# Pairwise bilinear products: the second tile of a two-tile x load is issued by GpSimd and placed on chosen DMA engines

## The chip, the cores and the metric

The kernel runs on one core of one Trainium2 chip. The metric is device time in microseconds (us). The time before is 1336.77 us, the median of three runs (1336.71 to 1336.96). A profiled execution has a span of 1335.1 us, counted from the first to the last instruction.

A core has five engines with their own instruction streams: TensorE (PE; its weight loads are listed apart as PEld), VectorE (DVE), ScalarE (ACT), GpSimd (POOL) and SyncE (SP). Sixteen DMA engines move data between HBM and the core's memory SBUF. SyncE, ScalarE and GpSimd can each issue transfers, and each has its own queue.

## The reference

The input has 4096 samples of 32 fields with 64 numbers each. For every pair of fields i < j (496 pairs) field i of each sample is multiplied by a 64 x 64 matrix that belongs to the pair, and the result is multiplied element by element with field j:

```python
i_idx, j_idx = np.triu_indices(32, k=1)
vi = inputs[:, i_idx, :]
vj = inputs[:, j_idx, :]
vdotw = jnp.einsum('bpd,pde->bpe', vi, W)     # W: (496, 64, 64)
return (vdotw * vj).reshape(B, -1)            # (4096, 31744) float32
```

All is float32. The output is 520 MB, the input x 33.6 MB, the weights 8.4 MB (with padding). So the kernel is mostly a stream of stores.

## The kernel before

The samples lie in 32 tiles (NT) of 128 rows, one row for each partition. For a tile, TensorE transposes x, multiplies each pair of fields (2p, 2p + 1) with the weights of all later fields into PSUM, and VectorE multiplies PSUM with x into a ring buffer in SBUF, from which SyncE stores. There are four stores in a tile, 7552, 6528, 7872 and 9792 columns wide; the ring has 28160 columns.

```python
STORES = [[0, 1], [2, 3], [4, 5, 6], [7, 8, 9, 10, 11, 12, 13, 14, 15]]
FIRST_HALF_AT, SECOND_HALF_AT = 9, 3
RING = 28160

def x_slots(NT):                       # which tiles are loaded together, and into which slot
    loads = [[(0, 0)]]
    for t in range(1, NT, 2):
        if t + 1 == NT:
            loads.append([(t, 1)])
        elif loads[-1][-1] == (t - 1, 2):
            loads.append([(t + 1, 0), (t, 1)])
        else:
            loads.append([(t, 1), (t + 1, 2)])
    return loads
...
    xbuf = const.tile([P, 3 * F * D], F32, tag="x", name="x")     # three slots of one tile
    def load_x(load):
        at = sum(len(before) for before in x_loads[: x_loads.index(load)]) * P * F * D
        n = len(load) * F * D
        s = load[0][1]
        nc.scalar.dma_start(
            out=xbuf[:, s * F * D : s * F * D + n],
            in_=x[at : at + P * n].rearrange("(p c) -> p c", p=P),
        )
...
    for t in range(NT):
        xt = slot[t]
        for load in x_loads:
            if min(load)[0] == t + 1:
                load_x(load)
        for s, group in enumerate(STORES):
            if at + store_w[s] > RING:
                at = 0
            osb = ring[:, at : at + store_w[s]]
            at += store_w[s]
            for p in group:
                if p == SECOND_HALF_AT:
                    transpose_x(xt, 1)
                if p == FIRST_HALF_AT and t + 1 < NT:
                    transpose_x(slot[t + 1], 0)
                ...                      # matmuls into PSUM, then on VectorE:
                        nc.vector.tensor_tensor(
                            runs(osb, o[0], o[1], n), runs(pm, 0, BANK, n), ..., ALU.mult)
            nc.sync.dma_start(
                out=out[:, t * cols + o0 : t * cols + o0 + store_w[s]], in_=osb
            )
```

x comes in 17 loads: tile 0 alone, fifteen loads of two tiles, and tile 31 alone. In a two-tile load each partition gets one run of 16 KB. The host lays x out so that each load is contiguous in HBM.

Of the kernel before, what the change touches and what calls it, by code (L numbers as in the profile page):

```python
# [1 line left out]

# [6 lines left out]

F32 = mybir.dt.float32  # L10
ALU = mybir.AluOpType

P = 128
BANK = 512
BANKS = 8

STORES = [[0, 1], [2, 3], [4, 5, 6], [7, 8, 9, 10, 11, 12, 13, 14, 15]]

LOADS = [[0], [1], [2, 3], [4, 5, 6], [7, 8, 9, 10, 11, 12, 13, 14, 15]]


FIRST_HALF_AT, SECOND_HALF_AT = 9, 3
RING = 28160


def x_slots(NT):
# [13 lines that stand above are left out]
@with_exitstack  # L40
def pair_bilinear_kernel(
    ctx: ExitStack,
    tc: tile.TileContext,
    x: bass.AP,
    w: bass.AP,
    out: bass.AP,
    F: int,
    D: int,
):

    nc = tc.nc
    NT = out.shape[1] * 2 // (F * (F - 1) * D)
    NPR = F // 2

    width = [(F - 1 - i) * D for i in range(F)]
    off = [sum(width[:i]) for i in range(F)]
    cols = sum(width)  # L80


    woff = [i % 2 * D + sum(width[i % 2 : i : 2]) for i in range(F)]
    store_w = [sum(width[2 * p] + width[2 * p + 1] for p in g) for g in STORES]

    const = ctx.enter_context(tc.tile_pool(name="const", bufs=1))
    psum = ctx.enter_context(tc.tile_pool(name="ps", bufs=1, space=bass.MemoryType.PSUM))

    ident = const.tile([P, P], F32, tag="ident", name="ident")
    make_identity(nc, ident)  # L90

    def runs(tl, a, b, n):

        ap = tl[:, a : a + n]
        return bass.AP(ap.tensor, ap.offset, [list(ap.ap[0]), [b - a, 2], list(ap.ap[1])])

    xbuf = const.tile([P, 3 * F * D], F32, tag="x", name="x")
    x_loads = x_slots(NT)
    slot = {t: xbuf[:, ts(s, F * D)] for load in x_loads for t, s in load}

    def load_x(load):

        at = sum(len(before) for before in x_loads[: x_loads.index(load)]) * P * F * D
        n = len(load) * F * D
        s = load[0][1]
        nc.scalar.dma_start(
            out=xbuf[:, s * F * D : s * F * D + n],
            in_=x[at : at + P * n].rearrange("(p c) -> p c", p=P),
        )

    pring = psum.tile([P, BANKS * BANK], F32, tag="pring", name="pring")
    bank = 0

    def take_banks(n):

        nonlocal bank
        if bank + n > BANKS:
            bank = 0
        got = pring[:, bank * BANK : (bank + n) * BANK]
        bank = (bank + n) % BANKS  # L120
        return got

    xT = const.tile([P, NPR * P], F32, tag="xT", name="xT")

    def transpose_x(xt, g):

        n = 2 * BANK // P
        pt = take_banks(2)
        for c in range(n):
            nc.tensor.transpose(pt[:, ts(c, P)], xt[:, ts(n * g + c, P)], ident)  # L130
        nc.scalar.copy(xT[:, ts(g, 2 * BANK)], pt)  # L131

    ring = const.tile([P, RING], F32, tag="ring", name="ring")
    at = 0

    load_x(x_loads[0])
    w_sb = const.tile([P, sum(width[0::2])], F32, tag="w", name="w")
    done = 0
    for g in LOADS:

        upto = woff[2 * g[-1]] + width[2 * g[-1]]
        nc.sync.dma_start(out=w_sb[:, done:upto], in_=w[:, done:upto])
        done = upto

    transpose_x(slot[0], 0)
# [10 lines that stand above are left out]
            o0 = off[2 * group[0]]  # L156
# [5 lines that stand above are left out]
                first = (width[2 * p] - 1) % BANK + 1  # L162
                for c1 in range(first, width[2 * p] + 1, BANK):
                    n = first if c1 == first else BANK
                    c0 = c1 - n
                    odd = width[2 * p + 1] and c1 > D
                    pm = take_banks(2)
                    for h in range(1 + bool(odd)):
                        a = woff[2 * p + h] + c0 - h * D
                        nc.tensor.matmul(  # L170
                            pm[:, h * BANK : h * BANK + n],
                            xT[h * D : (h + 1) * D, ts(p, P)],
                            w_sb[h * D : (h + 1) * D, a : a + n],
                            start=True,
                            stop=True,
                        )
                    xj = xt[:, (2 * p + 1) * D + c0 : (2 * p + 1) * D + c1]
                    o = [off[2 * p + h] - o0 + c0 - h * D for h in range(2)]
                    if odd and (c0 or c1 < width[2 * p]):
                        nc.vector.tensor_tensor(  # L180
                            runs(osb, o[0], o[1], n),
                            runs(pm, 0, BANK, n),
                            bass.AP(xj.tensor, xj.offset, [xj.ap[0], [0, 2], xj.ap[1]]),
                            ALU.mult,
                        )
                    else:
                        for h in range(1 + bool(odd)):
                            nc.vector.tensor_tensor(  # L188
                                osb[:, o[h] + h * D : o[h] + n],
                                pm[:, h * (BANK + D) : h * BANK + n],  # L190
                                xj[:, h * D :],
                                ALU.mult,
                            )
            nc.sync.dma_start(
                out=out[:, t * cols + o0 : t * cols + o0 + store_w[s]], in_=osb
            )


# [30 lines left out]
```

## Time and profile before

| | before |
|---|---|
| time, median of three | 1336.77 us |
| span of the profiled execution | 1335.1 us |
| DMA traffic | 562.87 MB in 21659 packets, mean 422 GB/s |
| stores, a tile | four, 3264 to 4896 KB, median 17.7 to 18.6 us from issue to landing |
| two-tile x load | 2048 KB, median 20.4 us from issue to landing |
| GpSimd | 0.7 us busy, no transfers |

How to read the lines that follow. In the list of busy times each engine has its time, the share of the span and the number of instructions. In the line of slices the span is cut into 40, and each digit is the busy share in tenths. A DMA queue has packets, MB and the time that its packets took as a share of sixteen engines' span. The chain is the work that ended last, followed back from the end. In the list of waits a line names who waited for whom, then the total in us, how often, and the longest. In a table of windows each row is a stretch of the span: its length, the busy time of PE, PEld, DVE, ACT and POOL with the number of instructions, the granted TensorE clock, the share of time in which DMA engines were busy, and GB/s.

### The profile page before, as it was taken

The page shows a single profiled execution, that of the slowest core. Times are in us where ns is not written, and L with a number is a line of the kernel's source. Part 1 is how long each engine was busy: PE and PEld are TensorE (multiplying, and loading weights), DVE is VectorE, ACT ScalarE, POOL GpSimd, SP SyncE. Part 2 cuts the span into 40 slices and gives each one's busy share as a digit, 9 for nine tenths or more (in the row PEclk, how much of TensorE's full clock was granted, in tenths as well). Part 3 has the DMA queues.
Part 4 walks back from the last instruction along what each step waited for, and adds up shares of the span by engine and source line. Part 5 has one row for each costly group of instructions (what it writes and reads, how often), then busy time and mean ns, then how long its engine had stood idle before and what let it go on. Part 6 is the DMA issues. An engine that isn't in the chain of part 4 may idle for free.

```text
span 1335.1 us, 13080 instructions
## 1 busy us (share of the span) xinstructions
PE 1160.6 (87%) x5376; PEld 544.9 (41%) x5376; DVE 1183.4 (89%) x1376; ACT 66.1 (5%) x65; POOL 0.7 (0%) x6
## 2 busy tenths in 40 slices
PE   6998989989899898998989889798998979989893
PEld 3443334443344443444444444344443434354441
DVE  5998989989899898998989899898998989989894
ACT  0000000000000000000000000000000000000000
POOL 0000000000000000000000000000000000000000
PEclk9999999989899999998989999899999999989997
DMA  9999999999999999999999999999999999999998
GB/s 397 433 430 430 431 428 430 418 433 430 413 425 410 436 414 427 426 414 433 405 432 431 419 429 411 432 426 421 428 413 430 426 407 417 429 421 423 429 425 352
DMA packets 21659, 562.87 MB, mean 422 GB/s; under 512 B 2400, under 2 KB 2400, under 8 KB 2656
## 3 DMA queue, kind: packets, MB, share of 16 engines
q1 hardware_dynamic: 19152, 528.49, 92.8%
q10 hardware_dynamic: 2448, 33.56, 5.9%
q8 instruction: 42, 0.69, 0.2%
q14 instruction: 17, 0.14, 0.0%
HBM read 41.94 MB, written 520.09 MB: 421 GB/s over the span
## 4 chain that ended last, share of the span: by engine, by line
DMA 47%; DVE 38%; issue 9%; PE 5%; DVEq 0%; ACT 0%
DMA out_dram<-ring 46%; DVE ring L180 32%; DVE ring L188 5%; PE pring L170 5%; DMA x<-in_x_dram 1%; DVEq L180 0%; PE pring L130 0%; ACT xT L131 0%; DVEq L225 0%; DVEq L188 0%
## 5 line engine op out<-in xcount | busy, mean ns | idle before, releaser
L170 PE MATMUL pring<-w,xT 64*128 64x512 f32 (+4 forms) x4864 | 1098.4, 564 | 146.4 <-DVE ring L180 133.5
L180 DVE TENSOR_TENSOR ring<-pring,x 128x1024 f32<-128x1024 f32 (+3 forms) x1056 | 1104.1, 1108 | 131.4 <-DMA out_dram<-ring 102.6
L170 PEld LDWEIGHTS pring<-w,xT 64*128 64x128 f32 x4864 | 489.3, 191 | 711.7 <-DVE ring L180 533.0
L131 ACT COPY xT<-pring 128x1024 f32<-128x1024 f32 x64 | 64.8, 1012 | 1224.1 <-PE pring L130 1224.1
L188 DVE TENSOR_TENSOR ring<-pring,x 128x64 f32<-128x64 f32 (+3 forms) x320 | 97.7, 356 | 2.6 <-DMA out_dram<-ring 1.9
L130 PEld LDWEIGHTS pring<-ident,x 128*128 128x128 f32 x512 | 55.6, 142 | 58.8 <-DVE ring L180 50.2
L130 PE MATMUL pring<-ident,x 128*128 128x128 f32 x512 | 70.8, 282 | 8.6 <-DMA x<-in_x_dram 8.6
L131 ACT ACT_TABLE_LOAD x1 | 1.3, 1283 | 1.7 <-PEq L221 1.7
masks.py:199 POOL TENSOR_SCALAR_AFFINE_SELECT ident<-ident 128x128 f32<-128x128 f32 x1 | 0.3, 292 | 0.1
masks.py:197 POOL MEMSET ident<- 128x128 f32 x1 | 0.2, 204 | 0.3 <-POOLq L221 0.3
L221 POOL MEMSET const-bfloat16-1.0<- 128x1 bf16 x1 | 0.1, 101 | 0.0
L221 POOL MEMSET const-uint8-127<- 128x1 uint8 x1 | 0.1, 101 | 0.0
L221 POOL MEMSET const-float32-0.0<- 128x1 f32 x1 | 0.1, 98 | 0.2 <-issue 0.2
L221 POOL MEMSET const-float32-1.0<- 128x1 f32 x1 | 0.1, 98 | 0.0
## 6 DMA issues: line engine op xcount, KB each, us to landing
out_dram<-ring SPq DMA_DIRECT2D x32, 4896.0 KB, 17.7
out_dram<-ring SPq DMA_DIRECT2D x32, 3936.0 KB, 18.1
out_dram<-ring SPq DMA_DIRECT2D x32, 3776.0 KB, 18.3
out_dram<-ring SPq DMA_DIRECT2D x32, 3264.0 KB, 18.6
x<-in_x_dram ACTq DMA_DIRECT2D x15, 2048.0 KB, 20.4
w<-in_w_dram SPq DMA_DIRECT2D x1, 2592.0 KB, 28.1
x<-in_x_dram ACTq DMA_DIRECT2D x2, 1024.0 KB, 12.8
w<-in_w_dram SPq DMA_DIRECT2D x1, 2016.0 KB, 22.2
```

Of the source, the lines that this page charges most:

```text
L130: nc.tensor.transpose(pt[:, ts(c, P)], xt[:, ts(n * g + c, P)], ident)
L131: nc.scalar.copy(xT[:, ts(g, 2 * BANK)], pt)
L170: nc.tensor.matmul(pm[:, h * BANK : h * BANK + n], xT[h * D : (h + 1) * D, ts(p, P)], w_sb[h * D : (h + 1) * D, a : a + n], start=True, st ...
L180: nc.vector.tensor_tensor(runs(osb, o[0], o[1], n), runs(pm, 0, BANK, n), bass.AP(xj.tensor, xj.offset, [xj.ap[0], [0, 2], xj.ap[1]]), ALU ...
L188: nc.vector.tensor_tensor(osb[:, o[h] + h * D : o[h] + n], pm[:, h * (BANK + D) : h * BANK + n], xj[:, h * D :], ALU.mult,)
L221: nc = bacc.Bacc("TRN2", target_bir_lowering=False, num_devices=1)
```

## The change

Thirteen of the fifteen two-tile loads, those whose second tile is 2, 4, ..., 26, are split. Their odd tile still comes from ScalarE. The even tile is issued by GpSimd in two transfers: 120 rows that are to lie on fifteen DMA engines, all but engine 4, and the last 8 rows on two engines, a pair that rotates from load to load. [...]so small transfers of k rows ("nudges", 16-byte pieces into a scratch tile that nothing reads) are put ahead of them to move the start to where it is wanted. The idea behind it is that one of the sixteen DMA engines has other work besides and should carry less of x.

```diff
+DMA_ENGINES = 16
+LIGHT = 4
+LIGHT_TILES = range(2, 28, 2)
+PAIRS_FROM = [6, 8, 10, 12, 14, 0, 1]
+HEAD = P - P % (DMA_ENGINES - 1)      # 120 rows
+REST = (P - HEAD) // 2                # 4 rows for each of two engines
+PAD = 16
...
+    def from_pool(out, in_):
+        tc.keep_in_program_order(nc.gpsimd.dma_start(out=out, in_=in_))
+
+    def from_engine(e):
+        nonlocal cursor
+        k = (e - cursor) % DMA_ENGINES
+        if k:
+            nudge = nudges[e == LIGHT + 1]
+            from_pool(
+                nudge[:k].rearrange("p (h c) -> p h c", h=2)[:, :, :4],
+                x[: k * 8].rearrange("(p h c) -> p h c", p=k, h=2),
+            )
+        cursor = e
+
+    def load_beside(at, xt, lap):
+        nonlocal cursor
+        n = F * D
+        from_engine(PAIRS_FROM[lap % len(PAIRS_FROM)])
+        g = REST * n + PAD
+        tail = x[at + HEAD * n : at + HEAD * n + 2 * g].rearrange("(g c) -> g c", g=2)
+        from_pool(xt[HEAD:], tail[:, : REST * n])
+        cursor += 2
+        from_engine(LIGHT + 1)
+        from_pool(
+            xt[:HEAD].rearrange("p (h c) -> p h c", h=2),
+            x[at : at + HEAD * n].rearrange("(h p c) -> p h c", h=2, p=HEAD),
+        )
+        cursor = LIGHT
+
     def load_x(load):
-        at = sum(len(before) for before in x_loads[: x_loads.index(load)]) * P * F * D
-        n = len(load) * F * D
-        s = load[0][1]
-        nc.scalar.dma_start(
-            out=xbuf[:, s * F * D : s * F * D + n],
-            in_=x[at : at + P * n].rearrange("(p c) -> p c", p=P),
-        )
+        at = sum(x_sizes[: x_loads.index(load)])
+        parts = [[(t, s)] for t, s in load] if any(t in LIGHT_TILES for t, s in load) else [load]
+        for part in parts:
+            t, s = part[0]
+            n = len(part) * F * D
+            if t in LIGHT_TILES:
+                load_beside(at, slot[t], LIGHT_TILES.index(t))
+            else:
+                nc.scalar.dma_start(
+                    out=xbuf[:, s * F * D : s * F * D + n],
+                    in_=x[at : at + P * n].rearrange("(p c) -> p c", p=P),
+                )
+            at += P * n + (2 * PAD if t in LIGHT_TILES else 0)
```

The host's layout of x follows (not shown): of an even tile the 120 rows are stored as two halves of 4 KB a row, the 8 rows as two blocks of four rows with 16 numbers of padding behind each. TensorE, VectorE and SyncE have the same instructions in the same order as before; ScalarE has 17 x loads as before, thirteen of them half as large; GpSimd has 52 transfers that it did not have.

More of the change, by code (lines that the diff above doesn't have):

```diff
@@ L98, in pair_bilinear_kernel @@
     x_loads = x_slots(NT)
+    x_sizes = [
+        sum(P * F * D + (2 * PAD if t in LIGHT_TILES else 0) for t, s in load) for load in x_loads
+    ]
     slot = {t: xbuf[:, ts(s, F * D)] for load in x_loads for t, s in load}
-    def load_x(load):
-        at = sum(len(before) for before in x_loads[: x_loads.index(load)]) * P * F * D
-        n = len(load) * F * D
-        s = load[0][1]
-        nc.scalar.dma_start(
-            out=xbuf[:, s * F * D : s * F * D + n],
-            in_=x[at : at + P * n].rearrange("(p c) -> p c", p=P),
-        )
+    nudges = [const.tile([DMA_ENGINES, 16], F32, tag=f"nudge{i}", name=f"nudge{i}") for i in range(2)]
+    cursor = 0
+    def from_pool(out, in_):
[24 more added lines that the diff above has]
+        cursor = LIGHT
+    def load_x(load):
+        at = sum(x_sizes[: x_loads.index(load)])
[11 more added lines that the diff above has]
+            at += P * n + (2 * PAD if t in LIGHT_TILES else 0)
     pring = psum.tile([P, BANKS * BANK], F32, tag="pring", name="pring")
@@ L209 @@
     rows = r_inputs.reshape(P, NT, F * D)
-    x = np.concatenate([rows[:, [t for t, _ in load]].ravel() for load in x_slots(NT)])
+    x = []
+    for load in x_slots(NT):
+        tiles = [t for t, _ in load]
+        if not any(t in LIGHT_TILES for t in tiles):
+            x.append(rows[:, tiles].ravel())
+            continue
+        for t in tiles:
+            if t in LIGHT_TILES:
+                x.append(rows[:HEAD, t].reshape(HEAD, 2, -1).transpose(1, 0, 2).ravel())
+                tail = np.zeros((2, REST * F * D + PAD), rows.dtype)
+                tail[:, : REST * F * D] = rows[HEAD:, t].reshape(2, -1)
+                x.append(tail.ravel())
+            else:
+                x.append(rows[:, t].ravel())
+    x = np.concatenate(x)
     wt = np.transpose(L0_rec_W, (1, 0, 2))
```

## The prediction

> **What bounds the kernel now.** I read the page's busy times first, then the DMA slices and queues, then the chain and the list of waits, and last the waits and windows cut into stages.
>
> ```profile
> PE 1160.6 (87%) x5376; PEld 544.9 (41%) x5376; DVE 1183.4 (89%) x1376; ACT 66.1 (5%) x65; POOL 0.7 (0%) x6
> DMA  9999999999999999999999999999999999999998
> q1 hardware_dynamic: 19152, 528.49, 92.8%
> q10 hardware_dynamic: 2448, 33.56, 5.9%
> q8 instruction: 42, 0.69, 0.2%
> ...
> DMA 47%; DVE 38%; issue 9%; PE 5%; DVEq 0%; ACT 0%
> ```
>
> VectorE is busy for 1183.4 of 1335.1 us, so some 150 us are left over; the DMA engines are in use from the first slice to the last. The store queue q1 and the x queue q10 take 98.7% of sixteen engines' span. The chain agrees: its largest part is the stores. So the bound is the DMA engines, and what counts is how evenly the work lies on the sixteen. The queue list has the hint: q8 is not data but instruction blocks, 42 of 16 KB, and 0.69 MB over TensorE's 2 x 5376 instructions is 64 bytes each.
>
> The list of waits, in two stages, shows how much room VectorE has. First 41 to 205 us (four tiles), then 205 to 1312 us (27 tiles):
>
> ```profile
> DVE ring L180 <- DMA out_dram<-ring: 13.0, 6, 5.1
> ...
> DVE ring L180 <- DMA out_dram<-ring: 89.7, 38, 6.2
> ```
>
> VectorE waits 3.3 us a tile for stores to leave the ring in both. A tile takes 40.8 us on average in the second stage (worked out below), so without these waits VectorE would need 37.5. The same stages as windows of two tiles each, with the cost of a pair of tiles:
>
> ```profile
> 40.00:120.20 80.20, 70.73 (x330) 32.57 (x328) 72.82 (x86) 4.05 (x4) 0.00 (x0) 0.98 1.00 431
> 206.00:287.60 81.60, 71.62 (x336) 33.13 (x335) 73.56 (x87) 4.05 (x4) 0.00 (x0) 0.96 1.00 426
> ```
>
> The last column is GB/s: 431 early, 426 later, with the busy share 1.00 in both. That share cannot resolve one or two per cent, so I went to the packet records of the trace. Each store ends in sixteen 4-byte semaphore packets, one for each engine; in order of time they show who is behind. The first store of tiles 0, 4, 16 and 31, in us:
>
> ```
> tile   8th engine   15th engine   last engine
>  0        38.86         39.43         40.39
>  4       199.24        202.32        202.65
> 16       690.98        692.31        694.58
> 31      1300.60       1301.64       1304.74
> ```
>
> Early the engines run together. From tile 5 on exactly one is far behind, 3 to 4 us in every store, while most of the others end within 0.2 us of each other. It gets no further behind because the ring then makes the other fifteen wait for it: VectorE may not overwrite a ring region before all sixteen engines have left it.
>
> Its extra work fits q8. By the 8th engine, tiles 0 to 4 take 160.38 us, 40.10 us a tile; tiles 4 to 31 take 1101.36 us, 40.79 us a tile. A pair of tiles then costs 81.6 us against 80.2. There are 42 instruction blocks in 16 pairs, 2.6 a pair; at the 0.611 us that a 16 KB x packet takes this is 1.6 us. The match says that one engine carries all of q8. The records do not number the engines; that it is engine 4 is the change's claim.
>
> [...]
>
> [...]
>
> [...]
>
> **The change part by part.** Removed: in 13 of 15 two-tile loads the second tile no longer goes over all sixteen engines from ScalarE. Every engine carried 8 rows of 8 KB of it. Engine 4 now carries none: 13 x 64 KB, and at 8 x 309 ns (the duration of an 8 KB x packet in the records) that is 2.47 us a load, 32 us in all. It had 42 x 0.611 = 26 us too much. So it stops being the last, with a margin that it can use up during the last five tiles, which are loaded as before.
>
> Moved: the 120 rows put the same 8 rows on each of fifteen engines. The other 8 rows go to a pair, 4 rows or 32 KB each, 1.2 us; the pairs rotate. Over thirteen loads engines 6 to 15 and 0 get two shares (2.4 us), engine 1 three (3.6 us), engine 2 one, engines 3 and 5 none.
>
> Added: smaller packets. A row of two tiles was one packet of 16 KB, 611 ns. Now it is one of 8 KB (309 ns) and two of 4 KB, which from 611 and 309 (7 ns plus bytes at 27.1 per ns) I estimate at 158 ns each: 8 x (309 + 316 - 611) = 0.11 us a pair, 1.5 us in all. The 26 nudges touch 199 engine slots with two 16-byte pieces each; a 32-byte packet takes 7 ns in the records, so below 0.1 us an engine, and even at ten times that 1 us. GpSimd issues 52 transfers; it was idle throughout.
>
> Waits: GpSimd's load of an even tile waits only for the tile that last used its slot, which is done one tile earlier than ScalarE's joint load could go. The transposes need it more than one tile (40 us) later, against 20.4 us to landing now. So it is off the path, also if each GpSimd issue costs some us.
>
> The sum: the 27 tiles from 4 to 31 contain 25 tiles' worth of x load instead of 27, 2 x 64 KB an engine or 4.9 us less. At the early rate they would take 27 x 40.10 - 4.9 = 1077.8 us against 1101.4: 23.6 us saved. At the end the last store waits for engine 4 from 1331.20 (15th) to 1333.70 (16th): 2.5 us saved. Costs: 1.5 packets, 2.4 to 3.6 shares of rows, some 1 nudges and semaphores: about 5.5 us. 1336.8 - 26.1 + 5.5 = 1316.2. I add 1 us for leftover imbalance: 1317 us.
>
> **The rivals.**
>
> Wrong engine: the cursor does not start at zero, or counts otherwise. Then fifteen engines include the loaded one and another is skipped. The loaded engine keeps its 64 KB, gains a share or two of 32 KB (2.4 us) and smaller packets: 1337 to 1342 us. For it speaks that no trace shows the placement and everything rests on the start of the cursor; against it, that the change is written so exactly around it. One in six.
>
> Half given back: fifteen engines become the bound and GpSimd's transfers cost them more than 1.5 us, [...]because the 4 KB packets take more than 158 ns, or because a third queue disturbs the order in which stores are served. At 0.5 us more a load this is 6.5 us: 1323 us. One in four.
>
> VectorE becomes the bound. Without waits for stores it would need 37.5 us a tile, 75 a pair, against the 80.2 us that the DMA engines need. In the first four tiles the DMA ran at full rate with VectorE as it is. I give this little.
>
> Hidden anyway: the fetch engine's lag would not count if the ring were deep enough. The saturated lag and the 81.6 us against 80.2 speak against it.
>
> **Range and chances.** The ceiling of the gain is 26 us, 1310.7 us, just above the 2% line at 1310.0. To pass it the early stage itself must have been held back a little (its 80.2 us a pair against 79.9 us for 2.16 MB an engine at 27.05 bytes per ns). Working placement gives 1311 to 1325, wrong placement 1337 to 1342. A range of 1309 to 1335; faster by over 2% 0.11, within 2% 0.85, slower by over 2% 0.04, for a GpSimd path that stalls the kernel in a way I do not see.
>
> **What would show it.** In the queue list a third queue with 13.6 MB and some 4,450 packets (3,224 of data, 398 of nudges, 832 semaphores), and q10 down to 19.9 MB with 2,448 packets as before. GB/s near 430 in the middle slices instead of 426. In the semaphore packets no single engine 3 to 4 us behind; a pair of tiles at 80.3 to 80.6 us by the 8th engine. VectorE's wait for the stores falls from 104.5 us by about 20. If instead one engine is still 3 to 4 us behind in every store, the placement failed. If all run together and a pair still costs over 81 us, the GpSimd transfers ate the gain. If a wait of TensorE or VectorE for x appears, my reading of the slots was wrong.

## The result and the profile after

The changed kernel takes 1326.1 us, the median of four runs (1325.03 to 1327.1), against 1336.81 us: a ratio of 0.9919, 95% interval 0.9905 to 0.9933. That is 10.7 us less. The prediction was 1317 us (1309 to 1335): the direction and the means are as foreseen, the gain is about half of the 19.8 us forecast.

The page of the changed kernel, in the views shown of the kernel before: busy times, DMA in 40 slices with GB/s, the queues (packets, MB, share of sixteen engines' span) and the chain.

```profile
PE 1166.4 (88%) x5376; PEld 551.2 (42%) x5376; DVE 1184.7 (89%) x1376; ACT 66.1 (5%) x65; POOL 32.5 (2%) x58
DMA  9999999999999999999999999999999999999998
GB/s 326 436 425 429 431 432 432 427 432 423 431 433 429 431 427 431 427 430 433 425 430 425 427 432 424 433 426 431 430 426 433 430 430 431 429 422 437 427 422 357
q1 hardware_dynamic: 19152, 528.49, 93.3%
q10 hardware_dynamic: 2448, 19.92, 3.6%
q0 software_dynamic: 5408, 13.65, 2.7%
q8 instruction: 42, 0.69, 0.2%
...
DMA 49%; DVE 34%; issue 7%; PE 7%; DVEq 0%; SPq 0%
```

A third queue, q0, carries the thirteen even tiles, 13.65 MB. The middle slices are near 430 GB/s. The first slice is not: 326 GB/s, against 397 before, with the engines shown as fully busy. That is one thing I had not foreseen. The same list of waits as before, from 205 to 1312 us, and the same windows of a pair of tiles in the middle:

```profile
DVE ring L232 <- DMA out_dram<-ring: 68.3, 37, 6.4
```

```profile
206.00:287.60 81.60, 73.87 (x344) 36.03 (x340) 75.06 (x88) 4.05 (x4) 2.43 (x4) 0.96 1.01 430
```

VectorE's waits for the ring fall from 89.7 to 68.3 us in this stretch, and the same 81.6 us carry 430 GB/s instead of 426. The semaphore packets that end each store, first store of four tiles, in us:

```
                   before                                   changed
tile   8th engine  15th engine  last engine    8th engine  15th engine  last engine
 0        38.86       39.43        40.39           44.08       45.63        45.85
 4       199.24      202.32       202.65          205.50      206.66       206.98
16       690.98      692.31       694.58          689.28      691.37       692.22
31      1300.60     1301.64      1304.74         1290.27     1292.45      1294.51
```

VectorE waits for the last of the sixteen: in the kernel before it goes on at 276.04 us, 0.58 us after the sixteenth of these packets of the store that it waits for (275.46) and 2.4 us after the fifteenth (273.65).

The lone laggard is gone in the middle: in the first stores of tiles 5 to 31 the last engine is on average 0.58 us behind the 15th, before 2.38 us. Tiles 4 to 31 take 1084.8 us instead of 1101.4, so 16.6 us are gained there. But the first store is 5.2 us later, and at tile 31 a laggard is back, 2.1 us behind.

### The profile page after: what moved, and what is told of

Same layout as the page of the kernel before. It is cut to its first block, busy times and chain, and to the rows that moved or that the text cites. A ratio compares the mean times of both kernels' runs of the same rounds, so it can differ in the third digit from the quotient of the medians.

```text
span 1325.0 us, 13175 instructions
## 1 busy us (share of the span) xinstructions
PE 1166.4 (88%) x5376; PEld 551.2 (42%) x5376; DVE 1184.7 (89%) x1376; ACT 66.1 (5%) x65; POOL 32.5 (2%) x58
## 3 DMA queue, kind: packets, MB, share of 16 engines
q0 software_dynamic: 5408, 13.65, 2.7%
## 4 chain that ended last, share of the span: by engine, by line
DMA 49%; DVE 34%; issue 7%; PE 7%; DVEq 0%; SPq 0%
DMA out_dram<-ring 48%; DVE ring L232 30%; PE pring L222 7%; DVE ring L240 4%; DMA w<-in_w_dram 2%; DVEq L232 0%; PE pring L182 0%; SPq L194 0%; DVEq L291 0%; DVEq L240 0%
## 5 line engine op out<-in xcount | busy, mean ns | idle before, releaser
L232 DVE TENSOR_TENSOR ring<-pring,x 128x1024 f32<-128x1024 f32 (+3 forms) x1056 | 1105.3, 1108 | 116.0 <-DMA out_dram<-ring 78.2
L222 PEld LDWEIGHTS pring<-w,xT 64*128 64x128 f32 x4864 | 495.3, 191 | 691.7 <-DVE ring L232 511.8
L117 POOL DMA_DIRECT2D x<-in_x_dram x26 | 17.2, 663 | 912.3 <-DVE ring L240 912.3
L117 POOL DMA_DIRECT2D nudge<-in_x_dram x26 | 14.7, 567 | 3.9 <-DMA nudge<-in_x_dram 3.7
```

What stands on the lines that cost most here:

```text
L117: tc.keep_in_program_order(nc.gpsimd.dma_start(out=out, in_=in_))
L222: nc.tensor.matmul(pm[:, h * BANK : h * BANK + n], xT[h * D : (h + 1) * D, ts(p, P)], w_sb[h * D : (h + 1) * D, a : a + n], start=True, st ...
L232: nc.vector.tensor_tensor(runs(osb, o[0], o[1], n), runs(pm, 0, BANK, n), bass.AP(xj.tensor, xj.offset, [xj.ap[0], [0, 2], xj.ap[1]]), ALU ...
```

## The experiments

Twelve kernels. All times are medians, and each ratio is against runs of the kernel before on the same chip.

| kernel | us | ratio (95% interval) |
|---|---|---|
| GpSimd loads for tiles 4 to 26 | 1320.79 | 0.9879 (0.9864 to 0.9894) |
| GpSimd loads for tiles 4 to 30 | 1318.66 | 0.9865 (0.9850 to 0.9879) |
| plan rotated, engine 8 left out | 1347.39 | 1.0077 (1.0062 to 1.0092) |
| plain GpSimd loads, sixteen engines | 1337.63 | 1.0005 (0.9997 to 1.0014) |
| tile 2 in halves, from ScalarE | 1321.03 | 0.9883 (0.9869 to 0.9896) |
| tile 2 in halves, from GpSimd, sixteen engines | 1321.55 | 0.9887 (0.9874 to 0.9901) |
| the same, with nudges ahead | 1322.64 | 0.9895 (0.9879 to 0.9912) |
| tile 2 on fifteen engines, no nudges | 1325.85 | 0.9925 (0.9910 to 0.9941) |
| more instructions, kernel before | 1342.42 | 1.0041 (1.0027 to 1.0055) |
| more instructions, GpSimd tiles 4 to 30 | 1321.72 | 0.9885 (0.9871 to 0.9898) |
| fewer matmuls, kernel before | 1939.40 | 1.4508 (1.4486 to 1.4530) |
| fewer matmuls, GpSimd tiles 4 to 30 | 1939.53 | 1.4509 (1.4488 to 1.4531) |

### Is it the start and the end, or a toll on each load?

```diff
-LIGHT_TILES = range(2, 28, 2)
+LIGHT_TILES = range(4, 28, 2)
```

> Tile 2 comes from ScalarE together with tile 1 as in the kernel before; the twelve even tiles 4 to 26 stay with GpSimd on chosen engines. Theory (the start): the changed kernel ran 1326.1 us instead of 1316 mainly because its first GpSimd load lies among the weight loads, whose packets then take longer (739 ns instead of 498 for 13 KB), and the 8th engine ends the first store at 43.3 us instead of 38.9. Then this kernel gains 4 to 5 us back: 1321 to 1322.5 us, first store near 39 us. Rival (a toll on each load): every GpSimd load costs some 0.7 us more than estimated. Then leaving out one of thirteen changes next to nothing: 1325.5 to 1327 us.

Measured: 1320.79 us, 5.3 us less than the changed kernel, and the 8th engine ends the first store at 38.97 us. The theory of the start holds; a toll on each load of GpSimd would have left the time where it was.

```diff
-LIGHT_TILES = range(2, 28, 2)
+LIGHT_TILES = range(4, 32, 2)
```

> Tile 2 from ScalarE, the fourteen even tiles 4 to 30 from GpSimd on chosen engines. Theory (the start and the end): besides the 4 to 5 us of the start, the loaded engine is no longer alone at the end: in the changed kernel it is 2.1 us behind the 15th engine in the first store of tile 31 because the loads of tiles 27 to 31 use all engines. Expected 1318.5 to 1320.5 us. Rival (a toll on each load): 1325.5 to 1327.5 us, one load more than in the changed kernel.

Measured: 1318.66 us, 2.1 us less again. From the 8th engine in the first store of tile 31 to the last engine in its last store it is now 30.5 us (1284.64 to 1315.16); before and in the changed kernel it was 33.1 and 33.2. So the two even-tile loads at the end that still used all sixteen engines, those of tiles 28 and 30, cost 2 to 3 us. This is the fastest version of all that ran.

### Is it engine 4, and does the cursor start at zero?

```diff
-LIGHT = 4
-PAIRS_FROM = [6, 8, 10, 12, 14, 0, 1]
+LIGHT = 8
+PAIRS_FROM = [10, 12, 14, 0, 2, 4, 5]
```

> The same plan rotated by four engines: the 120 rows leave out engine 8 in place of engine 4, and the pairs rotate with it. Theory (engine 4 carries the instruction blocks, and the cursor starts at 0): the lag of 3 to 4 us in each store returns, and the time is that of before plus the start (4 us) plus packets and two shares of rows: 1340 to 1345 us. Rival (the gain comes from loading the two tiles at different times, not from the engine): about 1326 us.

Measured: 1347.39 us, 21 us slower than the same plan four engines away, and slower than the kernel before. In the first stores of tiles 5 to 31 the last engine is 2.74 us behind the 15th on average; VectorE's waits for the ring are back:

```profile
DVE ring L232 <- DMA out_dram<-ring: 98.1, 48, 5.9
```

The changed kernel has 78.2 us on this line over the span. So the placement works: the engine that the kernel counts as 4 is the loaded one, and leaving out the one counted as 8 does not help. Whether the kernel's count from zero is also the chip's cannot be told from this, since the records number no engine; that count 4 hits the loaded one is what the two runs show. That the 120 rows leave an engine out shows in the packet records of the changed kernel: in 11 of the 13 such loads a line of other packets, each begun within 20 ns of the end of the one before, runs from the first 4 KB packet to the last. Of the 15 loads of 8 KB packets from ScalarE in the same kernel one has such a line, of the 15 two-tile loads before none. The time is 2.4 us above my range. The first store is 4.7 us late, and a tile costs 40.95 us against 40.79 before, 4.3 us over 27 tiles: together 1346 us. The remaining 1.4 us I cannot place.

The other half of the question: does it help at all that the tiles come apart, by another queue?

```diff
-        (8 rows on a pair of engines, 120 rows on fifteen, nudges ahead of both)
+        from_pool(xt, x[at : at + P * F * D].rearrange("(p c) -> p c", p=P))
```

> The same thirteen even tiles from GpSimd, each in one plain transfer of 128 rows of 8 KB, no nudges, all engines alike. Theory (balance): nothing is balanced, one engine lags by 3 to 4 us again: 1336 to 1342 us, the lower end if packets of 8 KB do not hold up the weight loads. Rival (loading at different times brings the gain): 1324 to 1328 us.

Measured: 1337.63 us; the interval of the ratio holds 1. In the first stores one engine is 2.42 us behind the 15th on average. Issuing from GpSimd costs nothing that can be measured here and by itself brings nothing. In the loads at the start, the weight packets of 13 KB take 498 ns, as before.

### What slows the start down?

In the changed kernel's first 10 to 20 us, where the weights, ScalarE's x and GpSimd's first load come together, the packet records show the weight packets of 13,312 bytes at 739 ns on average, before at 498; those of 16,128 bytes at 792 instead of 603. GpSimd's own 4 KB packets take 225 ns there and 160 ns beside the stores later. The windows, 10 to 20 and 20 to 30 us, of the kernel before, of the changed kernel and of the one with tiles 4 to 26 (last columns: granted clock, DMA busy share, GB/s):

```profile
10.00:20.00 10.00, 8.90 (x39) 4.08 (x37) 6.09 (x6) 1.01 (x1) 0.00 (x0) 1.00 1.02 433
20.00:30.00 10.00, 9.56 (x47) 4.05 (x46) 10.00 (x12) 1.01 (x1) 0.00 (x0) 1.00 1.03 423
```

```profile
10.00:20.00 10.00, 8.90 (x32) 4.74 (x33) 4.19 (x4) 1.01 (x1) 0.00 (x0) 1.00 1.04 314
20.00:30.00 10.00, 6.47 (x26) 3.01 (x24) 6.39 (x7) 0.00 (x0) 0.00 (x0) 0.75 1.02 331
```

```profile
10.00:20.00 10.00, 8.90 (x35) 4.01 (x35) 5.90 (x6) 1.01 (x1) 0.00 (x0) 1.00 1.01 431
20.00:30.00 10.00, 9.76 (x48) 4.19 (x46) 10.00 (x11) 1.01 (x1) 0.00 (x0) 1.00 1.02 416
```

Busy to the full in all three (1.01 to 1.04), but a quarter of the rate is gone in the changed kernel: a packet that takes 739 ns instead of 498 counts as busy for all of them. The changed kernel's TensorE pays with a wait of its own there, which the kernel before does not have:

```profile
PE pring L222 <- DMA w<-in_w_dram: 3.5, 1, 3.5
```

Candidates were the 4 KB packets, GpSimd's queue, the nudges, and the spread over fifteen engines. From the kernel with tiles 4 to 26 I changed the load of tile 2 alone:

```diff
-    (tile 2 in ScalarE's 16 KB packets together with tile 1)
+    o2 = slot[2].rearrange("p (h c) -> p h c", h=2)                        # two pieces of 4 KB a row
+    i2 = x[at : at + P * n].rearrange("(h p c) -> p h c", h=2, p=P)
+    nc.scalar.dma_start(out=o2, in_=i2)             # halves, from ScalarE
+    from_pool(o2, i2)                               # or: halves, from GpSimd
```

> From the kernel with GpSimd loads for tiles 4 to 26 (1320.8 us): tile 2 alone is loaded by ScalarE in the GpSimd layout, 128 rows in two pieces of 4 KB each. Theory A (packets of 4 KB from HBM beside the weight loads hold these up, whoever issues them): weight packets of 13 KB at 650 to 740 ns as in the changed kernel, 1324 to 1326 us. Theory B (GpSimd's queue holds them up): weight packets at 498 ns, 1320.5 to 1321.5 us.

> The same, but tile 2 in two pieces of 4 KB a row is issued by GpSimd, on all sixteen engines, with no nudge ahead of it. Both theories: weight packets near 700 ns and 1324 to 1327 us, since it has both, small packets and GpSimd's queue. If it runs as the kernel without it (1320.8 us), neither is the cause and what is left are the nudges, the 8 rows on two engines or the time at which the load comes, since the plain GpSimd load of 8 KB packets had the weights at 498 ns.

Measured: 1321.03 and 1321.55 us; weight packets of 13 KB at 498 ns in both. Both theories fell, also as a pair. On sixteen engines, 4 KB packets from GpSimd's queue do no harm. Two candidates were left:

```diff
+    from_engine(6); cursor = 8; from_engine(LIGHT + 1)    # nudges of 6 and 13 rows, then as above from GpSimd
```

```diff
-    from_pool(o2, i2)
+    from_pool(o2[:HEAD], i2[:HEAD])                       # 120 rows, meant for fifteen engines, no nudges
+    nc.scalar.dma_start(out=o2[HEAD:], in_=i2[HEAD:])     # the last 8 rows
```

> As the kernel that loads tile 2 by GpSimd in pieces of 4 KB on sixteen engines (1321.5 us, weight packets at 498 ns), with the changed kernel's first two nudges ahead of it. Theory A (fifteen engines[...]): the nudges are innocent, weight packets at 498 ns, 1321 to 1322.5 us. Theory B (the nudges set off the slow stretch): weight packets at about 730 ns, 1325.5 to 1327 us.

> The same, without nudges, but GpSimd loads only 120 rows of tile 2, so on fifteen engines[...]; the last 8 rows come from ScalarE. Theory A (fifteen engines): weight packets of 13 KB near 700 ns, 1324.5 to 1327 us. Theory B (nudges): weight packets at 498 ns, 1321 to 1322.5 us.

Measured: with nudges 1322.64 us and 498 ns; on fifteen engines 1325.85 us and 713 ns. From issue to landing, in us, the largest weight load tells the same story: before, with nudges, on fifteen engines, in the changed kernel.

```profile
w<-in_w_dram SPq DMA_DIRECT2D x1, 2592.0 KB, 28.1
```

```profile
w<-in_w_dram SPq DMA_DIRECT2D x1, 2592.0 KB, 28.3
```

```profile
w<-in_w_dram SPq DMA_DIRECT2D x1, 2592.0 KB, 32.6
```

```profile
w<-in_w_dram SPq DMA_DIRECT2D x1, 2592.0 KB, 34.7
```

So it is the fifteen engines. The stretch lasts as long as that load: in the kernel on fifteen engines the 120 rows have landed at 21.4 us, and weight packets of 13 KB that begin before that take 873 ns on average, those that begin later 515. The last 8 rows, which go apart in both slow kernels, are not what does it: in the changed kernel they have landed at 10.4 us, before the first of these weight packets begins, at 13.0 us. And it happens only beside other loads. Later the 120 rows lie beside stores alone and run at 160 ns a packet, 159 to 162 on average in each of the twelve loads. Why this is so, the runs do not show.

### Are the instruction blocks engine 4's additional work?

```diff
+                    if p % 2 == 0:
+                        nc.tensor.matmul(pm[:1, 0:1], xT[0:D, p * P : p * P + 1],
+                            w_sb[0:D, woff[2 * p] + c0 : woff[2 * p] + c0 + 1], start=True, stop=True)
                     for h in range(1 + bool(odd)):
```

> The kernel before, with one matmul of one column more ahead of every chunk of the even pairs p (20 a tile, 640 in all, each with its weight load): 1280 instructions more, 5 instruction blocks of 16 KB more; the products are the same. Theory (one DMA engine carries all instruction blocks and sets the pace): 5 x 0.611 = 3.1 us more, 1339.5 to 1340.5 us. Rival (the lag has another cause): 1336.8 to 1337.3 us, since TensorE has 4 us a tile to spare.

> The same additional matmuls in the kernel with GpSimd loads for tiles 4 to 30 (1318.7 us). Theory: engine 4 was relieved of 14 x 2.47 = 35 us against 26 us of blocks, so it takes 3 us more unnoticed: 1318.4 to 1319.5 us. Rival (the additional matmuls cost time on TensorE): as much more as in the other kernel, 1321 to 1322 us.

My count was too low: each matmul runs in two passes, so the 640 became 1280 with as many weight loads, and 10 blocks instead of 5, 52 where there were 42 (busy times and instruction queue of the kernel before with the addition):

```profile
PE 1243.6 (93%) x6656; PEld 538.5 (40%) x6656; DVE 1189.4 (89%) x1376; ACT 66.1 (5%) x65; POOL 0.7 (0%) x6
q8 instruction: 52, 0.85, 0.2%
```

10 blocks at 0.611 us are 6.1 us. Measured: 5.5 us more in the kernel before, but also 3.1 us more in the relieved kernel, with its runs spread over 3 us. There the last engine is only 0.42 us behind the 15th, so its 3.1 us are not a lag; TensorE is busy for 1237.7 us instead of 1162.3, and VectorE waits for it 28 us instead of 19. The addition thus has a cost on TensorE, and how much of the 5.5 us is that cost I cannot say. The last engine's pace rises from 40.82 to 40.99 us a tile, 0.17 us for 0.31 blocks, which would be 0.54 us a block. By its size that agrees with the theory; the packet records below show that it is not the blocks.

The opposite was to be cleaner: fewer matmuls, fewer blocks.

```diff
                     for h in range(1 + bool(odd)):
+                        if t and h:
+                            continue
```

From tile 1 on the second matmul of a chunk is left out, and VectorE multiplies what lies in that PSUM bank.

> The kernel before, in which from tile 1 on the second matmul of each chunk (h = 1) is left out, so VectorE multiplies what an earlier tile left in that PSUM bank: 1116 of 2432 matmuls fewer, which at two passes with a weight load each are 4464 instructions or 17.4 blocks of 16 KB of 42; all DMA data stay. Theory (the instruction blocks are engine 4's additional work): 17.4 x 0.611 = 10.6 us less, 1325.5 to 1327.5 us. Rival (engine 4 is slower for another reason): 1336.5 to 1337 us.

> The same matmuls left out of the kernel with GpSimd loads for tiles 4 to 30 (1318.7 us). Theory: its bound is the other fifteen engines, so fewer blocks on engine 4 change nothing: 1317.5 to 1319 us. Rival (TensorE's work is what counts): as much less as in the other kernel, 1308 us.

Measured: 1939 us in both. It failed as a test, since the bound became another one. The kernel before with fewer matmuls, a window early, one later (the third number from the end is the granted clock), and its busy times:

```profile
40.00:120.00 80.00, 77.06 (x162) 34.91 (x161) 58.37 (x68) 3.04 (x3) 0.00 (x0) 0.62 0.81 346
400.00:480.00 80.00, 79.50 (x127) 37.36 (x127) 53.34 (x62) 2.02 (x2) 0.00 (x0) 0.50 0.59 249
```

```profile
PE 1900.1 (98%) x3144; PEld 887.0 (46%) x3144; DVE 1249.6 (64%) x1376; ACT 66.1 (3%) x65; POOL 0.7 (0%) x6
```

TensorE's granted clock fell to 0.50 and stayed there (0.515 on average over the run), so TensorE became the bound with 3144 matmul instructions instead of 5376.

The packet records of the kernel before decide the question against the blocks. On one engine each packet begins as the one before it ends (97% of the store packets from 204 to 1289 us begin within 5 ns of the end of another), so the laggard's packets can be followed through a store. A stretch of tile 8, with the instruction block that falls into it:

```
start us    ns   packet                         its engine ends this store
 374.39   1194   store                          last
 375.10    879   instruction block, 16 KB
 375.58   1208   store                          last
 375.97   1578   store, begins as the block ends   14th
 376.79   1208   store                          last
 377.99   1199   store                          last
```

The other store packets here take 1166 ns. The block holds up a packet of another engine by 412 ns, and the laggard runs through it undisturbed. So it is with 24 of the 25 blocks that fall where no x load runs: the packet that begins as the block ends is 378 to 413 ns too long, and its engine is not the last in that store. (The 25th lies at 65 us, when the engines still ran together.) With the additional matmuls it is all 32 of 32 such blocks.

What the laggard has is something else: its eight packets of a store each take some 3% longer, 980 to 1030 ns at 26,112 bytes where the others take 968, about 32 ns a packet. It shows in 65 of the 69 stores of tiles 5 to 31 that no x load touches, each time on the last engine. The delay comes to 0.22 us a store without an instruction block and 0.25 us with one, 0.9 us a tile. That is its whole surplus: its packets of a tile, stores and half a two-tile x load, would take 39.9 us at the usual durations, and its pace is 40.82. With the additional matmuls, 15640 instructions instead of 13080, it is 37 ns a packet and 0.26 us a store, which gives 0.15 of the 0.17 us by which a tile grew. So the burden is larger with more instructions (in the relieved kernel too, 39 ns a packet instead of 33), but no packet in any queue of the records accounts for it; what it is stays open, also whether it comes with the recording itself.

The same mark finds the engine in the other kernels, in stores without an x load. In the rotated plan it is the last in 32 of the 33 stores of tiles 5 to 31 that show the mark. In the changed kernel it is never the last in tiles 5 to 24 (20 stores, 2.6 us ahead of the last on average) and the last in 6 of 8 stores of tiles 29 to 31. So the change did relieve the engine that lagged, and that engine is the one that comes back at the end.

## Why the prediction was half right

The bound and the laggard: right. One DMA engine set the pace, it is the one that the kernel counts as engine 4, and VectorE was not in the way: beside GpSimd's transfers its products of 1,024 columns take 1218 ns on average, before 1217.

The reason for the lag: wrong. "The match says that one engine carries all of q8" does not hold. The blocks fall on an engine other than the laggard, and the laggard's surplus is its slower packets, 0.9 us a tile or some 28 us in 32 tiles. That 42 blocks at 0.611 us give 26 us is a coincidence, and so the margin in the prediction, 32 us of relief against 26, came out about right by luck. The records also have the blocks' own durations, 0.97 us on average instead of 0.611. The forecast time does not rest on it, since the sum took its rate from the first four tiles, before the slower engine had fallen behind far enough to hold up the others.

The placement: right, though that 120 rows take fifteen engines was an assumption until the run. The rival "wrong engine", which I put at one in six, is what the rotated plan showed, 1347 us and not 1337 to 1342.

The rate: right. I had predicted a pair of tiles at 80.3 to 80.6 us by the 8th engine; it is 2 x 40.18 = 80.4. (The 27.05 bytes per ns behind my 79.9 us are those of the shortest 31,488-byte store packets before, 1164 ns.) In the stretch from tile 4 to 31 the sum gives 1077.8 us plus about 5 of costs, 1082.9; measured 1084.8. The 4 KB packets cost 160 ns against the 158 that I estimated, and q0 has the 3,224 data packets that I counted. The tiny ones are other than I had thought, 199 of 32 bytes for the nudges and 1,985 of 4 or 8 bytes instead of 398 and 832, but at 9 ns each they hardly matter.

The start: wrong, and the largest miss. The sum had no term for it. I wrote that GpSimd's load of an even tile "is off the path", with tile 2 treated like the others, and priced its packets by their durations beside stores. Tile 2's load lies among the weights, where 120 rows on fifteen engines stretch every packet: the first store is 5.2 us later, and leaving the load out of the placement brought 5.3 us back.

The end: wrong by its size. "At the end the last store waits for engine 4 ...: 2.5 us saved." Nothing was saved: from tile 31's first store to the end it takes 33.2 us, before 33.1. I had said that engine 4 had a margin which it "can use up during the last five tiles". It was used up before the end: from tile 29 on the engine with the slower packets was mostly the last again, and in the first store of tile 31 it was 2.1 us behind. With tiles 28 and 30 relieved too, that stretch takes 30.5 us.

The account, from the traces: 5.2 us at the start, 1.0 in tiles 0 to 4 (161.4 us by the 8th engine instead of 160.4), 1.9 in the middle and 2.6 at the end are 10.7 us, of which some 0.5 in tiles 0 to 4 was in the sum as a cost. To the end of the last store the traces have 10.2 us of gain where the sum had 20.6, so 10.4 are to be explained, and the account closes to within 0.2. (The traced run took 1327.1 us, 1.0 above the median.) A version without the two misses, tiles 4 to 30, ran 1318.66 us, 2.5 us above the sum for the changed kernel.

## What to carry to other kernels

When all DMA engines look busy, look at the semaphore packets that end a transfer. Here one engine was behind all the others, by 2.38 us on average in the first stores of tiles 5 to 31, VectorE waited 89.7 us from 205 to 1312 us for stores to leave the ring, and moving bytes off that engine was worth 18 us of 1337 with the best choice of tiles. Why that engine lags need not be known for it, and a sum that fits is no proof: follow the engine's packets one by one. Price a moved transfer in the company in which it will run: the same 120 rows on fifteen engines cost 5 us beside other loads and at most some 0.2 us a load beside stores (all that the sum leaves open in the middle, 1.9 us, over twelve loads). And relieve the engine to the very end of the kernel, since what it gained before is soon used up: here it was 2.6 us ahead in tiles 5 to 24 and mostly the last again from tile 29 on.

## What was not expected of the hardware

The DMA busy share does not fall when packets are held up. In the start of the changed kernel the DMA share is 1.02 to 1.04 at 314 to 331 GB/s; before it is 1.02 to 1.03 at 423 to 433.

A load spread over fifteen engines in place of sixteen stretched the packets of another load from 498 to 713 or 739 ns, though 120 rows on fifteen engines are 8 rows for each as before.

One DMA engine's store packets take some 3% longer than those of the other fifteen (980 to 1030 ns at 26,112 bytes where the others take 968), in the kernel before and in the changed one, and a little more when there are more instructions (37 ns a packet instead of 32). An instruction block of 16 KB falls on another engine and makes one store packet there 0.38 to 0.41 us longer.

Leaving out the second matmul of each chunk made the kernel 45% slower. In both versions the granted clock was 0.52 on average, with TensorE busy 98% of the time. The matmuls 512 columns wide that remain take 1037 ns on average, before 640. Why the clock is held at half the runs do not show.
